# Layers of the second and third chunk as one stream over two chunks of attention, in a transformer and state-space block

## The chip, the core and the metric

The kernel runs on one core of a Trainium2 chip. The core has five engines, each with its own instruction queue: TensorE (PE, matrix products, with weight loads shown apart as PEld), VectorE (DVE), ScalarE (ACT), GpSimd (POOL) and SyncE (SP, which issues most DMAs here). The metric is the device time in microseconds of one execution. The time before is the median of three runs, 1835.65 us.

## The reference

The input `x` has 2 batches of 1024 tokens and 256 features. Four layers follow one another, each on a layer norm of the running sum and added to it:

```python
x = x + attn(layernorm(x), Wq, Wk, Wv, Wo)        # 16 heads of 128, causal, ALiBi, scores clipped
x = x + ternary_ffn(layernorm(x), w_gu, w_pr)     # weights quantised to -1, 0, 1 times a group scale
x = x + mamba(layernorm(x), in_proj, conv, ...)   # 512 channels, 16 states each
x = x + kept_two_ffn(layernorm(x), wg, wu, wd)    # of every 4 hidden values the 2 largest are kept
```

The state-space layer (mamba) projects to 512 channels and a gate, convolves over four tokens, and then computes for every channel and each of 16 states the recurrence `h = exp(delta * A) * h + delta * B * x` along the tokens, and from it `y = sum over states of h * C`. The recurrence runs through all 1024 tokens of a batch.

## The kernel before

**Chunks.** The 2048 tokens are four chunks of 512 (`CH`): the first and second chunk are the two halves of the first batch, the third and fourth those of the second. A chunk has four tiles of 128 queries. Since attention is causal, the first and third chunk have short attention (at most 512 keys) and the second and fourth have long attention (640 to 1024 keys).

**Attention.** `attention()` (L382) is a generator that yields after every score tile: 16 heads by 4 tiles, 64 tiles a chunk. `load_head` (L262) issues a head's loads on SP while the head before it runs; keys and values of a batch's first half are written to DRAM and read back for its second half. `scores` (L355) multiplies queries by keys (L362), clips and masks them (L366, DVE), adds the ALiBi row and finds the minimum (L372, DVE's custom operation), and takes the exponential (L377, ACT). Two tiles later `turn` transposes the result on PE (L293), at a head's end `values` (L304) and `project` (L318, L324) follow. `qkv` (L328) of the next head is traced after the second tile of a head.

**Layers.** `ternary_ffn` (L451), `state_space` (L517) and `kept_two_ffn` (L885) of a chunk are generators too, chained by `rest(k)` (L947). The state space has 4 groups of 128 channels by 16 states, 64 *products* a chunk. Each takes a row of B and a row of C broadcast by DMA on SP, `delta * x * B` on POOL (`enter`, L736), the exponential on ACT (`decay`, L750), the scan along 512 tokens on DVE (`scan`, L757), the multiplication by C on POOL (`weigh`, L771), and an addition into the sum through PE's transposes (`total`, L701). These stages are staggered from one product to the next.

**Order.** A layer generator yields a number, the cost that its author puts on the step, after every step: 3 for a step of the ternary layer, 2.2 for a product, 4 for a step of the last layer, and so on. `cost(k)` (L952) is the sum for a chunk. The driver at the kernel's end (L970) advances attention of chunk `k` by one tile and then traces layers of chunk `k - 1` until their cost has reached the same share of the whole. What is left after the 64th tile is traced before the next chunk begins. So a *stage* is one chunk's attention with the layers of the chunk before it; the first stage has the quantisation of weights instead, and the fourth chunk's layers stand alone in a *tail*. The trace order is a preference: a planner puts each engine's instructions in order by it and by its own estimate of when operands are ready. The scans have one order written out: a scan is put behind the minimum (L372) of the score tile before the last (`pace["front"]`).

The third chunk's last projections (`held`) are not traced in its stage but between matmuls of the tail; the 4 steps of 4 units that `cost` counts for them are never yielded.

Of the kernel before, what the change touches and what calls it, by code (L numbers as in the profile page):

```python
# [17 lines left out]
P = 128  # L18
# [13 lines left out]
NU = S // U  # L32
# [9 lines left out]
def kernel(  # L42
# [28 lines left out]
    def bank(tag, bufs):  # L71
        return lambda name, dt=F32: ps.tile([P, 512], dt, tag=tag, name=name, bufs=bufs)
# [6 lines left out]
    CH = [(b, u) for b in range(B) for u in range(NU)]  # L79
    x = []  # L80
    for k in range(len(CH)):
        x.append(const.tile([P, UT, D], F32, name=f"x{k}"))

    def load_x(k):
        b, u = CH[k]
        src = x_in[b, u * U : (u + 1) * U, :].rearrange("(t p) d -> p t d", p=P)
        if k:
            nc.sync.dma_start(out=x[k], in_=src)
        else:

            for t in range(0, UT, 2):
                (nc.scalar if t else nc.sync).dma_start(out=x[k][:, t : t + 2, :], in_=src[:, t : t + 2, :])
# [19 lines left out]
    def layernorm_T(k, key, put, bank):  # L112
# [4 lines left out]
        step = 2 if k == len(CH) - 1 and key[0] != "a" else UT  # L117

        def turn_two(i):
            if i and step == 2:  # L120
                fill_in()
            tp = bank(f"lnp_{key}_{i}").rearrange("p (c t) -> p c t", c=KC)
            for j in range(2):
# [9 lines left out]
            put(slice(i * P, (i + 2) * P), tp)  # L133

        for i in range(UT):
# [3 lines left out]
            if (i + 1) % step == 0:  # L139
# [3 lines left out]
                for j in range(done.start, done.stop, 2):  # L143
                    turn_two(j)

    def plain(pool, key):
        xT = pool.tile([P, KC, U], F32, tag="xT", name=f"xT_{key}")
# [79 lines left out]
    def normed(k):  # L227
        xns[k], put = plain(a2, f"a{k}")
# [33 lines left out]
    def load_head(k, h):  # L262
        b, u = CH[k]
# [8 lines left out]
        n = (u + 1) * U  # L272
# [7 lines left out]
        if u:  # L280
            kd, vd = kept.pop((b, h))
            nc.sync.dma_start(out=w["kT"][:, :U], in_=kd)
            nc.sync.dma_start(out=w["v_all"][:, :UT, :], in_=vd)
        return w

    def turn(k, h, j, s, st):

        qi = CH[k][1] * UT + j
# [9 lines left out]
    def values(k, h, st):  # L298
        u = CH[k][1]
        zp = ps_z(f"z_{k}_{h}")  # L300
        last = (u + 1) * UT - 1
        for kb in range(last + 1):
            q0 = max(0, kb - u * UT) * P
# [4 lines left out]
        st["z"] = a2.tile([P, U], F32, tag="z", name=f"zs_{k}_{h}")  # L308
        nc.any.tensor_copy(st["z"], zp)  # L309

    def project(k, h, st):

        rr = a3.tile([P, UT], F32, tag="rr", name=f"rr_{k}_{h}")
        nc.vector.reciprocal(rr, st["rs"])
        for t in range(0, UT, 2):
# [12 lines left out]
    def qkv(k, h, st, xT):  # L328
        u = CH[k][1]
        st["qT"] = a2.tile([P, U], F32, tag="qT", name=f"qT_{k}_{h}")  # L330
        kT = st["kT"][:, u * U : (u + 1) * U]
        for n, dst, scale in (("q", st["qT"], -1.0 / math.sqrt(DH)), ("k", kT, 1.0)):
            pp = ps_mm(f"p{n}_{k}_{h}")
# [714 lines left out]
```

## Time and profile before

| what | value |
|---|---|
| median of three runs | 1835.65 us (1833.6 to 1840.51) |
| profiled execution, first to last instruction | 1836.9 us (its own time; the page lists nothing outside this span) |
| PE, DVE, ACT, POOL busy | 1718.3, 1218.3, 963.7, 832.2 us |
| first chunk's attention with quantisation | 0 to 225 us |
| second chunk's attention, first chunk's layers | 225 to 727 us, PE busy 480.3 |
| third chunk's attention, second chunk's layers | 727 to 1119 us, PE busy 354.2 |
| fourth chunk's attention, third chunk's layers | 1119 to 1604 us, PE busy 461.4 |
| tail, fourth chunk's layers | 1604 to 1837 us, PE busy 212.4 |
| POOL's two multiplications of a product (L736, L771) | 1356 and 1428 ns in the mean |
| DVE's scan (L757) | 1210 and 1269 ns |

Busy time is the time in which an engine executes something. Matrix products are pipelined, so PE's busy time counts the time with at least one in flight. The granted clock is a share of PE's full speed, and a window's figure is the mean over it. The stage ends were read off the score tiles and the layers' first and last instructions; a stage's work overlaps its neighbours' by a few microseconds.

### The profile page before, as it was taken

How to read it: one execution, taken by the hardware profiler on the slowest of the kernel's cores; microseconds unless marked ns; L12 is line 12 of the kernel's file. 1: busy time of each engine (PE TensorE's matmuls, PEld its weight loads, DVE VectorE, ACT ScalarE, POOL GpSimd, SP SyncE). 2: the span in 40 equal slices, each digit the busy share in tenths (PEclk: the TensorE clock that was granted, in tenths of full speed). 3: DMA queues.
4: the chain of work that ended last, by engine and by line, in shares of the span. 5: the costliest groups of instructions: out<-in, count | busy, mean ns of one | idle time of the engine just before them, and what ended most of it. 6: DMA issues, size and time to landing. Idle time of an engine off the chain costs nothing. (4 is left out here: it accounts for less than half of the span.)

```text
span 1836.9 us, 24217 instructions
## 1 busy us (share of the span) xinstructions
PE 1718.3 (94%) x7956; PEld 1144.2 (62%) x7956; DVE 1218.3 (66%) x2349; ACT 963.7 (52%) x1789; POOL 832.2 (45%) x674
## 2 busy tenths in 40 slices
PE   7999999998999999998888999999999999998899
PEld 4666666555656557755555667756656565566895
DVE  5666555777785473458886565557788655667975
ACT  3444474656563553555554545566555446446742
POOL 3324032588892000419998000418898500035870
PEclk9999999999999999999999999999999999999999
DMA  6443512466662311337787324227665430212541
GB/s 201 128 142 128 193 46 88 149 203 204 216 202 91 103 52 48 125 109 232 245 247 224 116 71 141 82 67 228 226 214 184 142 115 26 75 53 86 178 136 57
DMA packets 178301, 255.99 MB, mean 139 GB/s; under 512 B 16240, under 2 KB 90992, under 8 KB 177152
## 3 DMA queue, kind: packets, MB, share of 16 engines
q1 hardware_dynamic: 176752, 241.61, 41.4%
q0 software_dynamic: 1152, 12.58, 1.9%
q8 instruction: 63, 1.03, 0.2%
q14 instruction: 62, 0.51, 0.1%
q10 hardware_dynamic: 272, 0.26, 0.0%
HBM read 232.04 MB, written 22.35 MB: 138 GB/s over the span
## 5 line engine op out<-in xcount | busy, mean ns | idle before, releaser
L771 POOL TENSOR_TENSOR hc<-hs,cs 128x512 f32<-128x512 f32 x256 | 362.1, 1428 | 10.8 <-DVE ss L366 3.1
L362 PE MATMUL s<-kT,qT 128*128 128x512 f32 (+3 forms) x768 | 302.7, 495 | 19.9 <-DVE ss L366 18.0
L377 ACT ACTIVATE ss<-ss,nm 128x128 f32<-128x128 f32 (+7 forms) x256 | 198.8, 776 | 183.5 <-DVE nm L372 174.1
L366 DVE SCALAR_TENSOR_TENSOR ss<-s,lower 128x512 f32<-128x512 f32 (+3 forms) x384 | 204.6, 549 | 121.0 <-PE s L362 119.4
L736 POOL TENSOR_TENSOR db<-du,bs 128x512 f32<-128x512 f32 x192 | 259.2, 1356 | 44.4 <-DVE hs L757 30.6
L304 PE MATMUL z<-pT,v 128*128 128x512 f32 (+3 forms) x768 | 264.5, 492 | 10.9 <-ACT pT L296 10.2
L372 DVE CUSTOM_DVE_ANT_0 ss<-ss,alibi 128x128 f32<-128x128 f32 (+7 forms) x256 | 241.3, 945 | 3.5
L750 ACT ACTIVATE da<-dl,a_neg 128x512 f32<-128x512 f32 x256 | 177.9, 698 | 115.6 <-DVE hs L757 90.6
L304 PEld LDWEIGHTS z<-pT,v 128*128 128x128 f32 x768 | 142.8, 190 | 145.1 <-issue 92.7
L296 ACT COPY pT<-pt 128x512 f32<-128x512 f32 (+3 forms) x321 | 145.4, 474 | 162.0 <-PE pt L293 160.4
L293 PE MATMUL pt<-ident,ss 128*128 128x128 f32 x1152 | 180.3, 279 | 32.1 <-DVE x L324 18.5
L293 PEld LDWEIGHTS pt<-ident,ss 128*128 128x128 f32 x1152 | 140.0, 142 | 94.7 <-DVE x L324 33.0
L362 PEld LDWEIGHTS s<-kT,qT 128*128 128x128 f32 x768 | 127.9, 193 | 84.1 <-issue 43.4
L757 DVE TENSOR_TENSOR_SCAN hs<-da,db 128x512 f32<-128x512 f32 x128 | 153.8, 1210 | 38.6 <-ACT da L750 20.8
L757 DVE TENSOR_TENSOR_SCAN hs<-da,carry,db 128x512 f32<-128x512 f32 x128 | 159.1, 1269 | 24.4 <-POOL hc L771 14.7
L324 DVE SCALAR_TENSOR_TENSOR x<-o,rr,x 128x256 f32<-128x256 f32 x256 | 108.9, 476 | 76.7 <-PE o L318 76.5
L701 PE MATMUL y<-ident,hc 128*128 128x128 f32 x1024 | 144.8, 279 | 8.4 <-POOL hc L771 8.4
L342 PEld LDWEIGHTS pv<-wv,xT_a 128*128 128x128 f32 x1024 | 124.4, 192 | 37.1 <-issue 25.3
L342 PE MATMUL pv<-wv,xT_a 128*128 128x128 f32 x1024 | 125.8, 275 | 5.5 <-ACT zs L309 3.4
L701 PEld LDWEIGHTS y<-ident,hc 128*128 128x128 f32 x1024 | 121.0, 145 | 14.3 <-POOL hc L771 11.9
L318 PE MATMUL o<-wo,zs 128*128 128x256 f32 x512 | 125.4, 386 | 4.1 <-ACT kT L338 3.0
L335 PE MATMUL pq<-xT_a,wq 128*128 128x512 f32 x256 | 122.7, 601 | 0.7 <-ACT xT_a L148 0.7
(204 smaller groups left out, 2468.7 us busy)
## 6 DMA issues: line engine op xcount, KB each, us to landing
cs<-bcd SPq DMA_DIRECT2D x256, 256.0 KB, 3.8
bs<-bcd SPq DMA_DIRECT2D x192, 256.0 KB, 4.3
alibi<-alibi_d SPq DMA_DIRECT2D x32, 512.0 KB, 4.2
wq<-in_wqT_dram SPq DMA_DIRECT2D x64, 128.0 KB, 3.5
wk<-in_wkT_dram SPq DMA_DIRECT2D x64, 128.0 KB, 3.1
wv<-in_wvT_dram SPq DMA_DIRECT2D x64, 128.0 KB, 2.8
wo<-in_woT_dram SPq DMA_DIRECT2D x64, 128.0 KB, 2.8
alibi<-alibi_d SPq DMA_DIRECT2D x32, 256.0 KB, 3.6
```

The costliest lines, as they stand in the source:

```text
L293: nc.tensor.transpose(tp[:, i, :], s[:, (kb0 + i) * P : (kb0 + i + 1) * P], ident)
L304: nc.tensor.matmul(zp[:, q0:], lhsT=st["v_all"][:, kb, :], rhs=st["pts"][kb // 4][:, kb % 4, q0:], start=(kb == 0), stop=(kb == last),)
L342: nc.tensor.matmul(vp[:, t, :], lhsT=xT[:, c, t * P : (t + 1) * P], rhs=st["v"][:, c, :], start=(c == 0), stop=(c == KC - 1),)
L362: nc.tensor.matmul(sp[:, :n], lhsT=st["qT"][:, j * P : (j + 1) * P], rhs=st["kT"][:, k0 : k0 + n], start=True, stop=True,)
L366: nc.vector.scalar_tensor_tensor(s[:, k0 : k0 + n], sp[:, :n], CLIP, lower[:, S - W + k0 : S - W + k0 + n], op0=ALU.min, op1=ALU.max,)
L372: pace["tile"] = nc.vector.tensor_tensor_reduce(out=s[:, :W], in0=s[:, :W], in1=st["alibi"][:, :W], scale=1.0, scalar=3.0e38, op0=ALU.add, ...
L377: nc.scalar.activation(s[:, :W], s[:, :W], AF.Exp, bias=nm, scale=-1.0, accum_out=st["rs"][:, j : j + 1])
L701: nc.tensor.matmul(yTs[c][:, t * P : (t + 1) * P], lhsT=h[:, t * P : (t + 1) * P], rhs=ident, is_transpose=True, start=start and t == 0, s ...
L736: nc.gpsimd.tensor_tensor(db[i], du, brow.pop(i), ALU.mult)
L750: nc.scalar.activation(da[i], parts[c][0], AF.Exp, scale=a_neg[:, c, n : n + 1])
L757: nc.vector.tensor_tensor_scan(out=hs[i], data0=da.pop(i), data1=db.pop(i), initial=0.0 if first else carry[:, n, c : c + 1], op0=ALU.mult ...
L771: nc.gpsimd.tensor_tensor(hc[i], hs.pop(i), crow.pop(i), ALU.mult)
```

## The change

A product of the second, third and fourth chunk yields 3.5 in place of 2.2 (the first chunk's still 2.2), and `cost` counts it so. The layers of the first chunk are traced as before. The layers of the second and third chunk form one list, `units`, that is worked off across the third and the fourth chunk's attention without a break between them. Each of these two attention chunks takes a share of the summed cost in proportion to `work(k)`, a weight of its attention that grows with the number of keys: 16 x 228 for the third and 16 x 388 for the fourth. What is not traced when the third chunk's attention ends stays in the list. After the fourth chunk the list is emptied.

The rest of the diff writes chunks as (batch, first tile, number of tiles), so that widths follow the chunk; all four chunks keep four tiles. Keys and values of a batch's first half go to rows of one DRAM tensor as wide as the batch, in place of one that is as wide as the chunk. `normed` of the next chunk and `qkv` of the next head change places in the text; they are traced after different tiles.

```diff
-    CH = [(b, u) for b in range(B) for u in range(NU)]
+CH = [(b, t, UT) for b in range(B) for t in range(0, NT, UT)]
...
-        if u < NU - 1:
-            kd = dr.tile([P, U], F32, tag="kd", name=f"kd_{k}_{h}", bufs=H)
-            nc.sync.dma_start(out=kd, in_=kT)
...
+        if t0 + ut < NT:
+            if t0 == 0:
+                kept[b, h] = (
+                    dr.tile([P, S], F32, tag="kd", name=f"kd_{b}_{h}", bufs=H),
+                    dr.tile([P, NT, DH], F32, tag="vd", name=f"vd_{b}_{h}", bufs=H),
+                )
+            kd, vd = kept[b, h]
+            nc.sync.dma_start(out=kd[:, t0 * P : t0 * P + w], in_=kT)
+            nc.sync.dma_start(out=vd[:, t0 : t0 + ut, :], in_=v)
...
                 if i >= 0:
-                    yield 2.2
+                    yield PRODUCT(k)
...
+    PRODUCT = lambda k: 2.2 if k == 0 else 3.5
+
     def rest(k):
-        yield from ternary_ffn(k)
-        yield from state_space(k)
-        yield from kept_two_ffn(k)
+        part = CH[k][2] / UT
+        for layer in (ternary_ffn, state_space, kept_two_ffn):
+            for step in layer(k):
+                yield step * part
...
+    work = lambda k: H * sum(32 + 10 * (CH[k][1] + j + 1) for j in range(CH[k][2]))
+    units, done, later = [], 0.0, range(2, len(CH))
+
+    def layers(until):
+        nonlocal done
+        while units and done < until:
+            step = next(units[0], None)
+            if step is None:
+                units.pop(0)
+            else:
+                done += step
+
     for k in range(1, len(CH)):
-        r, done = rest(k - 1), 0.0
-        for i in range(H * UT):
+        units.append(rest(k - 1))
+        if k == 1:
+            share = cost(0)
+        else:
+            share = sum(cost(i - 1) for i in later) * work(k) / sum(work(i) for i in later)
+        begun, steps = done, H * CH[k][2]
+        for i in range(steps):
             next(heads)
-            whole = cost(k - 1)
-            while done < whole * (i + 1) / (H * UT):
-                done += next(r, whole)
-        for _ in r:
-            pass
+            layers(begun + share * (i + 1) / steps)
+        if k in (1, LAST):
+            layers(math.inf)
```

## The prediction

> **What bounds the kernel now.** I read the page's head first, then the busy times in windows cut at the stage ends (an attention chunk is a stage), then the windows inside the third and fourth chunk's attention, then how many score tiles lie in each, and last the groups and waits of the worst window.
>
> ```profile
> span 1836.9 us, 24217 instructions
> PE 1718.3 (94%) x7956; PEld 1144.2 (62%) x7956; DVE 1218.3 (66%) x2349; ACT 963.7 (52%) x1789; POOL 832.2 (45%) x674
> PE   7999999998999999998888999999999999998899
> POOL 3324032588892000419998000418898500035870
> ...
> 727.00:1119.00 392.00, 354.16 (x1617) 240.18 (x1616) 257.39 (x486) 199.76 (x399) 203.70 (x162) 0.97 0.52 165
> 1119.00:1604.00 485.00, 461.37 (x2017) 292.16 (x2015) 320.41 (x603) 267.36 (x459) 224.99 (x171) 0.99 0.43 139
> ...
> 727.00:830.00 103.00, 99.98 (x432) 64.57 (x430) 54.87 (x136) 55.40 (x109) 32.20 (x31) 1.00 0.34 113
> 830.00:1005.00 175.00, 141.91 (x709) 101.13 (x710) 143.53 (x209) 93.09 (x194) 169.24 (x130) 0.93 0.78 240
> 1005.00:1119.00 114.00, 112.27 (x477) 74.47 (x476) 58.99 (x142) 51.27 (x98) 2.26 (x2) 1.00 0.29 96
> 1119.00:1239.00 120.00, 118.35 (x481) 74.06 (x479) 66.94 (x144) 70.40 (x114) 31.68 (x33) 0.97 0.29 95
> 1239.00:1455.00 216.00, 198.45 (x965) 130.93 (x964) 174.70 (x308) 125.58 (x227) 190.28 (x136) 1.00 0.65 209
> 1455.00:1604.00 149.00, 144.57 (x575) 87.17 (x573) 78.77 (x154) 71.38 (x118) 3.03 (x3) 1.00 0.21 71
> ```
>
> In the window rows the columns are length, then busy us (and instructions) of PE, PEld, DVE, ACT and POOL, then clock, DMA share and GB/s. PE is busy for 94% of the span, and four of the six small windows have it at 97 to 99%. The hole is 830 to 1005, where the second chunk's state space runs beside the third chunk's short attention: PE idles 33.1 us of 175, its clock is granted at 0.93, and POOL is at 97%. The stretch 1239 to 1455 does the same products beside the long attention and loses 17.6 us; there no engine is full (PE 92%, POOL 88%, DVE 81%).
>
> ```profile
> L771 POOL TENSOR_TENSOR hc<-hs,cs 128x512 f32<-128x512 f32 x64 | 85.4, 1339 | 2.7 <-DMA cs<-bcd 2.7
> L736 POOL TENSOR_TENSOR db<-du,bs 128x512 f32<-128x512 f32 x60 | 81.2, 1356 | 2.3 <-DMA bs<-bcd 2.3
> L757 DVE TENSOR_TENSOR_SCAN hs<-da,carry,db 128x512 f32<-128x512 f32 x61 | 76.7, 1271 | 15.3 <-POOL hc L771 13.9 <-ACT da L750 1.4
> PE y L701 <- POOL hc L771: 7.9, 7, 3.0
> PE pt L293 <- DVE x L324: 8.0, 6, 2.4
> ```
>
> So in 830 to 1005 POOL's two multiplications per product set the pace, and PE waits for them (7.9 us) or for DVE, which does the scans ahead of the residual updates (8.0 us).
>
> **The change part by part.**
>
> *Trace order.* The layers of a chunk are units of cost given out per attention tile (64 tiles a stage). Before, the second chunk's layers cost 2.2 x 69 + 150.8 = 302.6 units, 4.73 per tile, which is 2.15 products per tile. The 150.8 are 35 (ternary layer), 30 (state space up to its products), 9 and 8 (inside and after them), 68.8 (last layer). With 3.5 per product the two chunks cost 392.3 and 395.8. The attention's weights are 16 x 228 and 16 x 388, so the third chunk's attention takes 37% of 788.1, or 291.7 units (4.56 per tile), and the fourth's 496.4 (7.76 per tile). The products thus go at 4.56 / 3.5 = 1.30 per tile beside the third chunk and 2.22 beside the fourth (before 2.16). The 65 units ahead of them take 14.3 tiles beside the third chunk (before 13.7; the trace has 16 score tiles up to 830, 30 in the hole, 18 after). At the end of that stage 217.7 units, 62 products, are issued, 57 of them added up. The rest of the second chunk's layers, about 100 units, moves into the first 13 tiles of the fourth chunk's attention.
>
> *Third chunk's attention.* The front stays 103 us with 16 tiles. The product stretch has 48 tiles in place of 30. A tile of short attention costs PE at most 150.6 / 46 = 3.27 us (60 to 215 us of the first chunk, with some weight transposes in it); I take 3.2. A product costs (141.9 x 0.93 - 30 x 3.2) / 64 = 0.56 us of PE. So PE: 48 x 3.2 + 57 x 0.56 = 186 us. POOL: 62 x (1.339 + 1.356) + 8 = 175. DVE: the attention rows of the window give 2.14 us a tile (custom operation 0.97, mask 0.47, update 0.45, small ones 0.25), 48 x 2.14 + 62 x 1.271 + 15 for step sizes = 197. Three engines come close together. PE at the 92% of 1239 to 1455 gives 202; DVE at the 97% that POOL reached gives 203. I take 203. Ends: 190 (PE at the 98% of 1005 to 1119) and 224 (DVE at the 88% that POOL had in the balanced stretch). Stage: 103 + 203 = 306 in place of 392, **-86 us**.
>
> A row speaks against the spreading. The score tile's custom operation (two SBUF inputs) took 1049 ns at 128x512 in the hole and 692 ns in 1005 to 1119, where POOL was idle; over the four widths the excess is 0.48 us, and 48 tiles now meet it in place of 30. It is inside the 2.14. The Trainium skill, "SBUF — State Buffer", section "Who interferes with whom", says that a VectorE instruction with two SBUF inputs and a GpSimd one that reads SBUF exclude each other for a whole instruction. As an estimate from that page, were every tile to wait out one whole POOL operation of 1.34 us, DVE would need 0.86 x 48 = 41 us more, the stretch 238 and the kernel 1847; the row has a third of that wait.
>
> *Fourth chunk's attention.* Moved in: window 1005 to 1119 less its attention, 112.3 - 18 x 3.2 = 54.7 us of PE, and seven products' additions, 4: **+58.5 us**, at the 98% that this work had. Its DVE (comparisons, masks) and one POOL power lie beside attention. Then the third chunk's layers start at tile 13 and run denser. Products are as dense as before (2.22 against 2.16), so that stretch keeps its loss. Their front, 65 units, has 8.4 tiles where it had 13.7: PE work 8.4 x 5.3 (a long tile: (198.5 - 34) / 31) + 48.8 (103 window less 16 tiles) = 93 us, and the same chain was done in 103 us from 727 to 830, so the products may lag some 10 us, two tiles. The third chunk's last projections are held for the tail, which leaves 16 units, two tiles, unused at the end. I take **+3 us**; ends 0 and +30 (a lag of six tiles more).
>
> *What else is issued.* The last layer's three weight loads (1 MB each, 4.9 to 9.9 us) and the ternary layer's two (8.7 and 11.7 us, POOL's queue) move behind the fourth chunk's head loads, and the row requests of the last products lie on SP between them. A head is loaded one head ahead, 24 to 30 us (four tiles of 392 / 64 or 485 / 64), which hides landings of 3 to 5 us; uncovered, a head's start would slip by that once or twice. The ternary loads still wait for the last layer's buffers, now beside attention. The third chunk's normalisation for the fourth (one 1.0 us POOL power) now queues behind products: 0 to 3 us, taken in the 203. Keys and values go to rows of one larger tensor, 2.3 and 2.5 us a write and 3.0 and 3.6 a read in as many requests: 0, hidden by the same lead. The widths by chunk, slices and the order of two calls on different tiles issue nothing new: 0. First two stages and tail: 0.
>
> **Sum.** 1836.9 (the profiled execution; the page shows nothing around the span, and it is 1.25 above the median) - 86 + 58.5 + 3 = 1812.4, so **1812**; the difference to the median is a tenth of a per cent and I leave it.
>
> **Rivals.**
> *Nothing but PE left (faster).* The long product stretch reaches 190 and the dense layers cost nothing: 1812 - 13 - 3 = 1796. For: windows at 98 to 99% wherever POOL is free. Against: three engines within 11 us of each other.
> *DVE takes POOL's place (no change).* The stretch takes 224: 1812 + 21 = 1833. For: the waits "PE pt <- DVE x" and the 81% balanced stretch that loses 17.6 us. Against: fewer scans per tile than in either stretch of before.
> *The dense fourth stage (slower).* The third chunk's layers, squeezed into 51 tiles, fall behind: with the lag beyond the two spare tiles, each further tile leaves work to be done after attention, where nothing covers it, at a long tile's 5.3 us. Six such tiles, +32, and 1844; from five tiles on the kernel is level with before. For: the chain's 103 us against 93. Against: attention tiles can be issued ahead in between.
>
> **How the numbers follow.** My forecast 0.50, the faster rival 0.20, level 0.16, slower 0.14. A change of 0.5% (9.2 us) is about what a measurement of this kernel tells from none. Faster: 0.70; same: 0.16; slower: 0.14. The likeliest case alone spans 1800 to 1824. For 8 in 10 the range takes in the faster rival and its unknowns down to 1788 and the level one up to 1840.
>
> **What the new profile would show.** The third chunk's attention ends near 1034, with about 48 tiles beside products, POOL at 85 to 90%, PE near 92% and fewer half-clock stretches. The fourth takes about 546 us, its first 13 tiles beside the second chunk's last layer, and products again at seven us a tile with PE near 92%. The prediction is wrong if DVE passes 95% in the long stretch, if PE idles ahead of the third chunk's products, or if layer work stands after the last attention tile.

## The result, and the profile after

The changed kernel takes 1849.88 us in the median (1847.15 to 1854.09, four runs), beside 1836.68 us of the kernel before (1833.6 to 1840.51) measured with it: a ratio of 1.0072, 95% interval 1.0053 to 1.0091. It is slower by 0.7%; 1812 us and a gain of 1.3% were forecast. The profiled execution took 1847.15 us, its span is 1845.4 us, so 33.0 us of the span are to be explained against the sum of 1812.4.

The head of the changed kernel's page, and its windows cut as those of before were (length, then busy us and instructions of PE, PEld, DVE, ACT and POOL, then clock, DMA share, GB/s):

```profile
span 1845.4 us, 24241 instructions
PE 1713.0 (93%) x7956; PEld 1140.7 (62%) x7956; DVE 1232.5 (67%) x2359; ACT 954.8 (52%) x1778; POOL 827.4 (45%) x674
PE   7999999998999999997988899999888999898899
POOL 3333031588891000408778500135987740035970
...
725.00:1057.00 332.00, 293.14 (x1410) 200.37 (x1409) 237.60 (x441) 177.62 (x372) 199.39 (x159) 0.98 0.58 182
1057.00:1614.00 557.00, 519.52 (x2224) 329.66 (x2222) 356.24 (x658) 280.82 (x475) 224.83 (x175) 0.99 0.39 128
...
830.00:1057.00 227.00, 190.74 (x961) 132.93 (x960) 180.76 (x289) 121.03 (x262) 171.79 (x132) 0.97 0.70 218
...
1272.00:1490.00 218.00, 190.25 (x896) 124.80 (x895) 168.34 (x290) 117.72 (x214) 183.31 (x133) 0.98 0.63 201
```

The work has moved as the change meant it to. The third chunk's attention takes 332 us in place of 392, the fourth's 557 in place of 485; together they are 12 us longer, and the first two stages and the tail are 4 us shorter. The other parts of the diff are at work in the second chunk's stage too, and that takes 495 us, 496 before: they are not what costs. POOL's row shows the saturated "9998" of the third chunk spread out to "8778". But nothing was won: in the long product stretch beside the third chunk, 830 to 1057, no engine is near full (PE 84%, DVE 80%, POOL 76%), and in the stretch beside the fourth chunk PE has fallen from 92% to 87%.

To compare stretches whose work differs I use one number of my own, the *loss*: the length of a stretch less the usual time of its matmuls. A product stretch runs from the first scan of a chunk to its last multiplication by C; what lies ahead of it in the stage is the front, what lies behind it the rear. The usual time of a matmul is the distance from its start to the next one's, read off the trace of before where the next follows at once (429 ns for 128x512, 216 ns for 128x256, 109 to 112 ns for 128x128; 230 and 120 ns for the faster number format). The stage borders are the last attention instructions here, a few us later than in the windows. The losses are good to some tenths of a us, the counts of score tiles to one.

| us | kernel before | kernel after |
|---|---|---|
| third chunk's stage: matmuls | 329.7 | 278.9 |
| its loss: front, products, rear | 4.2 + 51.3 + 3.1 = 58.6 | 5.9 + 47.4 + 0.5 = 53.8 |
| fourth chunk's stage: matmuls | 445.9 | 496.7 |
| its loss: front, products, rear | 7.0 + 24.1 + 7.7 = 38.8 | 5.1 + 38.3 + 12.2 = 55.6 |
| length of the two product stretches (score tiles) | 179.2 (30), 215.3 (31) | 228.3 (48), 224.7 (29) |

So 50.8 us of PE's work moved from the third stage to the fourth, and the loss went down by 4.8 us in the one and up by 16.8 us in the other. The 51 us of loss that the change was to win back stayed almost whole, though POOL was relieved. The loss contains time that PE worked at half clock: in the third chunk's product stretch 23.9 us stand at half clock before and 13.7 after, in the fourth's none and 6.8. If half of that time is lost, which is an estimate, the losses without it are 39 and 41 us in the third stage and 24 and 35 in the fourth; the little that the third stretch won would be clock. Whom PE waited for in the long stretch (waits of PE alone, us in total, times, longest):

```profile
PE z L312 <- ACT pT L304: 11.0, 5, 6.7
...
PE pt L301 <- ACT pT L304: 4.6, 1, 4.6
PE pt L301 <- DVE x L333: 4.6, 3, 2.1
PE pt L301 <- ACT ss L390: 3.9, 4, 1.3
```

The wait for POOL, "PE y <- POOL hc", was 7.9 us before and is gone; only a weight load still waits 0.4 us for that tile. In its place PE waits for the attention's own chain: transposed probabilities, exponentials and the residual. The same list for the stretch beside the fourth chunk, 1272 to 1490, and below it the two rows of 1239 to 1455 of the kernel before:

```profile
DVE ss L379 <- PE s L375: 40.6, 8, 10.9
...
POOL db L754 <- DVE hs L775: 19.9, 3, 6.9
```

```profile
DVE ss L366 <- PE s L362: 9.0, 11, 3.3
...
PE s L362 <- DVE ss L366: 7.8, 8, 1.3
```

There DVE now stands still for up to 10.9 us at a time until PE makes the next scores, 40.6 us in all against 9.0, with as many products and as dense as before. POOL's wait for the scans hardly changed (19.9 us, 17.1 before). Two questions follow: what holds PE in the long stretch if not POOL, and why equally dense products cost 14 us more beside the same long attention.

### The profile page after: what moved, and what is told of

It is laid out like the page before. It is cut to its first block, busy times and chain, and to the rows that moved or that the text cites. A ratio compares the mean times of both kernels' runs of the same rounds, so it can differ in the third digit from the quotient of the medians.

```text
span 1845.4 us, 24241 instructions
## 1 busy us (share of the span) xinstructions
PE 1713.0 (93%) x7956; PEld 1140.7 (62%) x7956; DVE 1232.5 (67%) x2359; ACT 954.8 (52%) x1778; POOL 827.4 (45%) x674
## 4 chain that ended last, share of the span: by engine, by line
PE 61%; DVE 16%; issue 8%; POOL 7%; ACT 4%; DMA 3%; SPq 0%; POOLq 0%; DVEq 0%; ACTq 0%
PE z L312 10%; PE s L375 7%; PE pv L352 5%; DVE hs L775 5%; PE pq L345 4%; PE pk L345 4%; PE o L327 4%; PE pt L301 3%; DVE ss L385 3%; PE in L626 3%; PE g_g L456 3%; PE u_g L456 3%; POOL hc L789 3%; DVE ss L379 3%; POOL db L754 2%
## 5 line engine op out<-in xcount | busy, mean ns | idle before, releaser
L789 POOL TENSOR_TENSOR hc<-hs,cs 128x512 f32<-128x512 f32 x256 | 356.1, 1408 | 41.2 <-PE y L719 30.9
L385 DVE CUSTOM_DVE_ANT_0 ss<-ss,alibi 128x128 f32<-128x128 f32 (+7 forms) x256 | 251.0, 983 | 3.8 <-DMA alibi<-alibi_d 0.3
```

Source lines behind the costliest of these rows:

```text
L385: pace["tile"] = nc.vector.tensor_tensor_reduce(out=s[:, :W], in0=s[:, :W], in1=st["alibi"][:, :W], scale=1.0, scalar=3.0e38, op0=ALU.add, ...
L789: nc.gpsimd.tensor_tensor(hc[i], hs.pop(i), crow.pop(i), ALU.mult)
```

## The experiments

"After" and "before" in the edits say which kernel was edited. Ratios are to the kernel before, measured beside it, with the 95% interval.

### The two halves of the change, and how the work is shared out

**The stream alone (after, edited).** Products weigh 2.2 everywhere again.

```diff
-    PRODUCT = lambda k: 2.2 if k == 0 else 3.5
+    PRODUCT = lambda k: 2.2
```

> The changed kernel with 2.2 per product everywhere: one stream over the third and fourth chunk's attention, products as cheap as before. Units: 302.6 + 304.8 = 607.4, of which the third chunk's attention takes 37%, 224.8 (3.51 per tile, 1.60 products per tile; 65 units of front take 18.5 tiles, so 45 tiles with products) and the fourth 382.6 (5.98 per tile, 2.72 products per tile). Theory 'spreading does not pay' (PE loses about as much per product stretch however long it is, and a denser fourth stage loses more): third stage near 335 us, the fourth's product stretch POOL-bound and losing more than 38 us, total 1845 to 1865. Rival 'the weight did the harm' (products held back into more tiles while other layers are squeezed): total 1825 to 1838.

Measured: 1877.03 us, 1.0199 (1.0172 to 1.0226). The third chunk's products lie beside 40 tiles (loss 47.1), the fourth's beside only 22, three to a tile, and there the loss is 62.6 us (37.5 us of the stretch stand at half clock). The total lies 12 us above the expected range; the third stage took 337 us, as expected. The row of that stretch, and its main wait:

```profile
1296.00:1512.00 216.00, 168.87 (x793) 111.98 (x793) 170.21 (x263) 104.04 (x186) 179.87 (x137) 0.91 0.61 193
```

```profile
PE pt L301 <- DVE x L333: 27.7, 4, 12.9
```

**The weight alone (after, edited).** Each chunk's layers are finished in their own stage again; products weigh 3.5.

```diff
-            share = sum(cost(i - 1) for i in later) * work(k) / sum(work(i) for i in later)
+            share = cost(k - 1)
...
-        if k in (1, LAST):
+        if True:
             layers(math.inf)
```

> The changed kernel with each chunk's layers kept to its own stage and emptied at its end, as before, but with 3.5 per product: 392.3 units over 64 tiles, 6.13 per tile, 1.75 products per tile in place of 2.15, the other layers 1.3 times as dense. Theory 'spreading does not pay': the third stage's product stretch takes more tiles (37) and more time, but its loss of some 50 us stays, so 1834 to 1842, level with before. Rival 'POOL's saturation is what cost PE': the stretch at 1.75 products per tile frees POOL and PE regains 15 to 25 us there, 1812 to 1825.

Measured: 1855.96 us, 1.009 (1.0072 to 1.0108), above both expected ranges. The second chunk's products are spread over 35 tiles beside the third chunk and lose 60.6 us, more than the 51.3 of 30 tiles; the fourth's over 36 tiles lose 25.9. Stream alone +2.0%, weight alone +0.9%, both +0.7%: the halves do not add up. The weight repairs part of what the stream does, by giving the fourth chunk's products 29 tiles in place of 22.

**Another share (after, edited).** The third chunk's attention takes 43% of the stream in place of 37%.

```diff
+            share = sum(cost(i - 1) for i in later) * {2: 0.43, 3: 0.57}[k]
```

> The changed kernel with one size altered: the third chunk's attention takes 43% of the two chunks' cost in place of 37% (338.9 units, 5.30 per tile, 1.51 products per tile; the fourth 449.2, 7.02 per tile, 2.01 products per tile). Theory 'the fourth stage is too dense': the product stretch beside the fourth chunk's attention covers 34 tiles in place of 29 and its loss of PE falls from 38 to about 25 us, the third's stays at 45 to 52: 1830 to 1840. Rival 'the split does not matter': within 5 us of the changed kernel, 1843 to 1853.

Measured: 1851.6 us, 1.0081 (1.0065 to 1.0097), in the range of "the split does not matter". The third chunk's products lose 46.8 us beside 41 tiles, the fourth's 34.6 beside 31. Between 30 and 48 tiles the third chunk's loss is 47 to 61 us in all of these kernels: how thinly the products are spread there hardly matters. (Two kernels further down, with 44 tiles and an even rhythm, lose 37 and 39 us.)

**Thinner products beside the fourth chunk (after, edited).** Only the third chunk's products weigh more, and the third stage keeps its share.

```diff
+    PRODUCT = lambda k: (2.2, 3.5, 4.5, 3.5)[k]
...
+            share = 291.7 if k == 2 else cost(1) + cost(2) - 291.7
```

> The changed kernel with 4.5 per product for the third chunk's layers alone, and the third chunk's attention keeping its 291.7 units: beside the fourth chunk's attention 566.4 units, 8.85 per tile, so 1.97 products per tile in place of 2.22, while the other layers there are 14% denser. Up to the fourth chunk's attention it is the changed kernel. Theory 'density of products in the fourth stage': its stretch loses 25 in place of 38 us, in all 1833 to 1842. Rival 'density of the other layers': the stretch gains what the front and the last layer lose, 1846 to 1858.

Measured: 1865.31 us, 1.0157 (1.0136 to 1.0179), above both expected ranges. With 31 tiles in place of 29 the fourth chunk's products lose 43.7 us, more than the 38.3 of the denser order, and 16.5 us are lost ahead of them. 20.5 us of that stretch stand at half clock (6.8 in the changed kernel); by the estimate above, 33 and 35 us are left without it. So thinner products alone do not bring the loss back to 24 us. (The second stage of this run was 7 us longer than that of the changed kernel with the same instruction order, which I cannot explain; the losses beside the fourth chunk don't contain it.)

### What holds PE in the long stretch

**DVE's second SBUF input (one edit, in both kernels).** The score tile's custom operation adds the ALiBi row and finds the minimum, from two SBUF inputs. Here a plain reduction with one input takes its place; the ALiBi row is left out of the computation.

```diff
-        pace["tile"] = nc.vector.tensor_tensor_reduce(
-            out=s[:, :W], in0=s[:, :W], in1=st["alibi"][:, :W], scale=1.0,
-            scalar=3.0e38, op0=ALU.add, op1=ALU.min, accum_out=nm,
-        )
+        pace["tile"] = nc.vector.tensor_reduce(nm, s[:, :W], AX.X, ALU.min)
```

In the kernel before:

> The kernel before, with the ALiBi row left out: the minimum of a score tile is taken by a reduction with one SBUF input in place of the custom operation with two. It serves as the base of the next run. Stretch of the second chunk's products: DVE's durations there should lose their excess of some 26 us. Theory 'exclusion of DVE and POOL': 1790 to 1815. Rival 'order of the queues': 1815 to 1835.

In the changed kernel:

> The changed kernel with the same ALiBi row left out. Theory 'exclusion of DVE and POOL costs the long stretch' (48 tiles meet POOL in place of 30, DVE's excess there 35 us against 26): without it the change gains, 15 to 30 us less than the kernel before without the row, and the third chunk's product stretch falls from 227 to about 200 us. Rival 'the queues' bursts' (score tiles of a head and scans take turns on DVE, POOL and PE wait in turns): the difference to the kernel before without the row stays between -5 and +20 us and the stretch at 215 us or more.

Measured: 1812.56 us, 0.9857 (0.9835 to 0.9878), with the kernel before edited, and 1818.07 us, 0.9887 (0.9864 to 0.991), with the changed one edited. The first lies in the range of the exclusion; the second lies 5.5 us behind it and its stretch at 213 us, between what the two theories said. Groups of the changed kernel in its long stretch, the custom operation with its 512 and 128 columns (count, busy us, mean ns), below them the same tiles with the reduction, and last the custom operation in 1005 to 1119 of the kernel before, where POOL is idle:

```profile
L385 DVE CUSTOM_DVE_ANT_0 ss<-ss,alibi 128x512 f32<-128x512 f32 x12 | 14.5, 1204 | 0.2
...
L385 DVE CUSTOM_DVE_ANT_0 ss<-ss,alibi 128x128 f32<-128x128 f32 x11 | 10.0, 905 | 0.3
```

```profile
L385 DVE TENSOR_REDUCE nm<-ss 128x1 f32<-128x512 f32 x12 | 8.1, 674 | 0.2
...
L385 DVE TENSOR_REDUCE nm<-ss 128x1 f32<-128x128 f32 x11 | 3.1, 281 | 0.2
```

```profile
L372 DVE CUSTOM_DVE_ANT_0 ss<-ss,alibi 128x512 f32<-128x512 f32 x5 | 3.5, 692 | 0.3
...
L372 DVE CUSTOM_DVE_ANT_0 ss<-ss,alibi 128x128 f32<-128x128 f32 x4 | 1.2, 293 | 0.1
```

With POOL idle the custom operation itself took 692 and 293 ns, so the reduction is only 2 to 4% cheaper, and nearly all of the difference (0.53 and 0.62 us here, 0.48 and 0.53 at the two widths between) is what the second input costs DVE beside POOL's work. I call it the exclusion of DVE and POOL. It makes 14 us for 30 tiles at 0.48 us and 25 for 47 at 0.53, not the 26 and 35 of the expectations. POOL's own multiplications change little: 1328 and 1360 ns beside the custom operation, 1296 and 1284 beside the reduction. The long stretch shrinks from 228 to 213 us (loss 47.4 to 32.3):

```profile
823.00:1036.00 213.00, 194.58 (x970) 137.46 (x971) 155.33 (x245) 121.18 (x263) 166.45 (x134) 0.95 0.68 213
1251.00:1467.00 216.00, 196.33 (x936) 130.65 (x935) 162.03 (x270) 120.64 (x220) 167.46 (x136) 0.98 0.60 187
```

In the kernel before, the short stretch only goes from 179 to 175 us (49.3 of loss left). So this exclusion costs 15 us in the long stretch of the changed kernel and 4 us in the full one of before (11 us in the kernel before beside the fourth chunk). It doesn't explain the fourth stage: there the stretches lose 13.4 us in the edited kernel before and 30.4 in the edited changed one, a difference of 17 against the 14 of the originals.

**Half of one POOL multiplication taken out (one edit, in both kernels).** `weigh` multiplies half of the tokens, and PE adds that half twice; the other half of the sum over states is left out.

```diff
-                nc.gpsimd.tensor_tensor(hc[i], hs.pop(i), crow.pop(i), ALU.mult)
+                    nc.gpsimd.tensor_tensor(hc[i][:, : w // 2], h[:, : w // 2], cr[:, : w // 2], ALU.mult)
...
-                        lhsT=h[:, t * P : (t + 1) * P], rhs=ident,
+                        lhsT=h[:, (t % 2 if half else t) * P : ((t % 2 if half else t) + 1) * P], rhs=ident,
```

In the kernel before:

> The kernel before with the multiplication by C over half of the tokens, as in the run with the changed kernel. POOL in the third chunk's stretch falls from 169 to about 130 us of 175. Theory 'POOL's saturation is only a small part of what PE loses there' (the waits that name POOL were 7.7 of 33 us): the stretch shrinks from 179 by 8 to 20 us, the other two by 4 to 8 us each, in all 1805 to 1822. Rival 'POOL's saturation was the whole loss': the stretch shrinks by 25 us or more, below 154, in all below 1805.

In the changed kernel:

> The changed kernel with the multiplication by C over half of the tokens (PE adds the half twice), which takes some 0.64 us of POOL per product away and leaves the scans whole. Theory 'chain on DVE': POOL's time is worth little, only the part in which it excludes DVE: third chunk's stretch 215 to 225 us, in all 1825 to 1842. Rival 'POOL still sets the pace of the products, through its buffers': third chunk's stretch below 212, fourth's below 212 us, in all below 1820.

Measured: 1813.14 us, 0.986 (0.984 to 0.9879), with the kernel before edited; 1824.27 us, 0.9917 (0.9893 to 0.994), with the changed one edited; the first as the theory had it, the second, with 213 us for its stretch, between theory and rival. The third chunk's product stretch of before, then the third's and the fourth's of after, with the lighter `weigh`:

```profile
822.00:988.00 166.00, 143.38 (x733) 104.01 (x733) 139.99 (x212) 95.49 (x196) 136.63 (x133) 0.93 0.84 260
```

```profile
831.00:1044.00 213.00, 189.41 (x970) 131.13 (x971) 171.29 (x292) 122.60 (x264) 139.34 (x134) 0.98 0.76 233
1258.00:1473.00 215.00, 193.40 (x937) 127.42 (x936) 167.73 (x299) 120.44 (x220) 149.52 (x137) 1.00 0.63 206
```

In the kernel before POOL loses a fifth of its time in the hole (169 to 137 us) and is no longer full (82%), yet the stretch only gets 13 us shorter and keeps 38.3 of its 51.3 us of loss. More than that POOL's saturation was not worth. In the changed kernel, where POOL stood idle for a quarter of the stretch, the same edit gives 15 us (47.4 to 32.4). A POOL that is far from full costs as much here as a full one. That DVE and PE wait their turn behind single POOL instructions would explain it, but was not tested by itself. Beside the fourth chunk the difference between the kernels falls from 14 to 9 us.

**Half of the scans taken out (one edit, in both kernels).** The scan runs over half of the tokens; `weigh` reads that half twice.

```diff
-                        out=hs[i], data0=da.pop(i), data1=db.pop(i),
+                        out=hs[i][:, : w // 2], data0=da.pop(i)[:, : w // 2], data1=db.pop(i)[:, : w // 2],
```

In the kernel before:

> The kernel before with the same half scans. Theory 'chain on DVE': its second and fourth chunk's stretches gain as in the changed kernel (12 and 10 us), the third chunk's little, since POOL's 169 us stay as the floor of its 175: 1805 to 1822, that is 5 to 20 us more than the changed kernel with half scans, so that the change would pay. Rival: it gains as much as the changed kernel or more and stays faster.

In the changed kernel:

> The changed kernel with the scans of the first three chunks over the first half of the tokens alone (the multiplication by C reads that half twice, so POOL, PE and ACT keep their work): DVE gets some 0.6 us per product less. Theory 'PE waits for the score tiles' chain on DVE, behind the scans': the product stretches (losses 24, 47 and 38 us) lose 12, 20 and 15 us less, in all 1790 to 1812, and the third chunk's falls from 228 to 205 us or less. Rival 'no single engine, any order does': less than 15 us in all, 1832 or more.

Measured: 1833.13 us, 0.9967 (0.9946 to 0.9989), with the kernel before edited, and 1836.0 us, 0.9985 (0.9972 to 0.9997), with the changed one edited: the chain on DVE was expected to give far more in both, and in the kernel before the third chunk's stretch even grew, from 179 to 184 us. DVE falls to 65% in the long stretch, which still loses 40.2 us:

```profile
825.00:1046.00 221.00, 195.45 (x972) 137.26 (x973) 143.11 (x297) 120.49 (x260) 173.96 (x133) 0.95 0.70 223
```

DVE's load is thus no bound there either: 38 us less work on it give 7. (23.9 us of that stretch stand at half clock in place of 13.7, so some 5 us of the gain went into clock.) Beside the fourth chunk the kernels lose 21.5 and 37.3 us, 16 apart.

**The transposes one tile later (after, edited).** `turn` follows its scores by three tiles in place of two, so that PE asks later for what ACT and DVE make.

```diff
-LAG = 2
+LAG = 3
```

> The changed kernel with a score tile's transposes three tiles after its scores in place of two (value products and projection one tile later as well): the chain of mask, minimum, exponential and copy gets one tile more, 4.4 us beside short attention. Theory 'latency of the chain': the waits of value products and transposes for it (some 20 us in the third chunk's stretch) shrink by half or more, 1822 to 1840. Rival 'buffers': score tiles, transposed tiles and the v buffer are held longer, and it is level or slower, 1845 to 1880.

Measured: 1893.69 us, 1.0293 (1.0274 to 1.0313), above both expected ranges. The first chunk's stage, where no products run, grew by 42 us; the long stretch lost 10 us less. The windows of the two:

```profile
0.00:279.00 279.00, 239.38 (x1028) 151.15 (x1029) 145.80 (x423) 106.38 (x265) 63.20 (x78) 0.96 0.42 132
892.00:1110.00 218.00, 194.15 (x975) 137.01 (x974) 180.78 (x299) 120.79 (x264) 173.46 (x133) 0.96 0.73 228
```

So the waits for the attention's chain are worth about 10 us in the long stretch and the edit is no cure. Whether the gains of exclusion, POOL's instructions and the chain add up was not tested. No single edit brought the loss of this stretch below 32 us, and what makes up the rest was not isolated.

### Why the fourth chunk's stretch got worse

**The next head's projections one tile later (one edit, in both kernels).** If the extra loss came from `qkv` and the products falling on the same tiles, moving the one should move the loss.

```diff
-            if j == ut // 2 - 1 and
+            if j == ut // 2 and
```

In the changed kernel:

> The changed kernel with the next head's query, key and value projections traced one tile later (after the third tile of a head), so that they no longer follow the head's value products in one block of PE work, 8 to 12 us without a score tile. Theory 'bursts': DVE no longer runs dry behind that block (pauses of 9 to 11 us before a mask, once in two heads), the product stretches lose 10 to 25 us less in all, 1822 to 1838. Rival 'the block is not the cause': 1843 to 1860, the projections come later and the next head's first scores wait for them.

In the kernel before (there the tile's number is 1, and becomes 2):

> The kernel before with the same move of the projections by one tile. Theory 'bursts': it gains too in its product stretches (losses 25, 51 and 24 us), 1815 to 1832; if it gains as much as the changed kernel, the block is a cost of both and not what the change lost. Rival: 1833 to 1850.

Measured: 1878.07 us, 1.0225 (1.0207 to 1.0244), and 1871.6 us, 1.0199 (1.0175 to 1.0224), both above all that was expected. All product stretches lose 1 to 9 us more in both kernels, and the difference beside the fourth chunk stays at 14 us (46.1 against 32.2). It tells nothing of the difference; the theory of one collision with the projections fell.

**The phase.** What was left was the order itself. A head has four tiles, and products come in groups of 16, one for each block of 128 channels, with one step of 3 units between. In the kernel before, a group costs 16 x 2.2 + 3 = 38.2 units; at 4.76 a tile (304.8 units of the third chunk's layers on 64 tiles) that is 8.0 tiles, two heads, and each group begins at the same place, 1.65 tiles after a head does (65 units ahead of the first make 13.65 tiles). In the changed kernel it costs 59 units; at 7.76 a tile that is 7.6 tiles, and its place drifts, from 1.35 to 0.2. Time, tiles and loss of each eight products (half a group) beside the fourth chunk, read off the two traces:

| kernel | us / tiles / loss of each eight products |
|---|---|
| before | 20/4/2.4, 32/4/3.9, 25/4/1.8, 32/4/4.6, 25/4/1.7, 32/4/4.6, 25/4/2.1, 22/2/2.6 |
| after | 20/3/3.9, 28/3/6.2, 34/5/5.0, 23/2/4.3, 36/5/5.2, 26/3/7.0, 36/5/3.8, 15/2/3.1 |

Four kernels tell density, drift and place apart. First, before with products at 2.4 in place of 2.2, so that the groups drift a little (8.3 tiles each, beginning at 1.05, 1.4, 1.7 and 2.0):

```diff
-                    yield 2.2
+                    yield 2.4
```

> The kernel before with 2.4 per product in place of 2.2 (in its costs too): 318.8 units a stage, 4.98 per tile, products 2.08 per tile in place of 2.16, and a group of 16 products with its step sizes takes 41.4 / 4.98 = 8.3 tiles in place of 8.0, so that it no longer falls on two heads. Theory 'rhythm' (the kernel before gains from a channel group every two heads, 8 products a head; any other pace makes the queues' order irregular): the second and fourth chunk's stretches lose 30 to 38 us each in place of 24, in all 1843 to 1862. Rival 'density': thinner products cost less, the stretches lose 20 to 24 us, 1830 to 1838.

Measured: 1855.78 us, 1.009 (1.0066 to 1.0113). The loss beside the fourth chunk is 28.5 us (before 24.1), beside the second 28.5 (24.9), beside the third 60.2 (51.3). The total is in the range of "rhythm", the losses beside the second and fourth chunk lie just below its 30 to 38.

Then the changed kernel with weights and share that make a group last 8.0 tiles again, so that it doesn't drift, but begin 3.2 tiles after a head does:

```diff
+    PRODUCT = lambda k: (2.2, 3.5, 3.524, 3.5)[k]
...
+            share = 314.7 if k == 2 else cost(1) + cost(2) - 314.7
```

> The changed kernel with its pace set to whole heads: the third chunk's attention takes 314.7 units (4.92 per tile; a group of 16 products takes 59 / 4.92 = 12.0 tiles, three heads), the fourth the rest, with 3.524 per product of the third chunk (7.42 per tile; a group takes 59.4 / 7.42 = 8.0 tiles, two heads). Theory 'rhythm': the fourth chunk's stretch loses about 24 in place of 38 us, the third's 35 to 47 in place of 47: 1818 to 1837. Rival 'the dense fourth stage, whatever its pace': losses stay at 34 us or more there, 1843 to 1855.

Measured: 1850.75 us, 1.0066 (1.0049 to 1.0083). The stretch loses 41.7 us: an even rhythm is not enough.

```profile
1266.00:1492.00 226.00, 197.11 (x910) 127.87 (x909) 172.60 (x295) 121.02 (x218) 190.22 (x136) 0.98 0.62 196
```

Next, the kernel before with the same density and rhythm, but its products two tiles later in the head (at 3.6):

```diff
-                    yield 2.2
+                    yield 2.53
...
-                yield 4
+                yield 24
```

(The 24 stand on the last step ahead of the products. `cost` counts both, which keeps 2.15 products to a tile and a group at 8.0 tiles beside the fourth chunk.)

> The kernel before with 20 units added ahead of the first product and 2.53 per product in place of 2.2 (costs too): 347.9 units a stage, 5.44 per tile, a group of 16 products in (16 x 2.53 + 3) / 5.44 = 8.0 tiles as before and 2.15 products per tile as before, but beginning at tile 15.6 in place of 13.7, so two tiles later within a head. Theory 'phase' (the rhythm of two heads helps only where the groups' ends fall at the right tile of a head): the second and fourth chunk's stretches lose 35 us or more each in place of 24, in all 1855 to 1875. Rival 'any rhythm of whole heads will do': 22 to 27 us each, 1833 to 1846.

Measured: 1896.9 us, 1.0302 (1.0273 to 1.0331). Beside the second chunk the loss goes from 24.9 to 44.2 us, beside the fourth from 24.1 to 40.4, beside the third from 51.3 to 66.5; the third's stretch and the fourth's have 33 and 32 tiles in place of 30 and 31. The losses are as "phase" had them; the total lies 22 us above its range. The fourth's stretch, and whom the engines wait for there:

```profile
1289.00:1527.00 238.00, 210.91 (x983) 138.58 (x982) 173.07 (x317) 126.87 (x227) 187.14 (x133) 0.97 0.57 180
```

```profile
DVE ss L366 <- PE s L362: 50.4, 13, 11.3
POOL db L736 <- DVE hs L757: 28.6, 8, 12.3
```

Nothing of the change is in this kernel, and yet it shows the changed kernel's picture: DVE stops for up to 11.3 us for the next scores (9.0 us in all in the kernel before, 40.6 in the changed one). Last, the changed kernel with even groups that begin 1.6 tiles into a head, as in before:

```diff
+    PRODUCT = lambda k: (2.2, 3.5, 3.007, 3.5)[k]
...
+            share = 314.7 if k == 2 else 408.9
...
-                done += step
+                done += step * (0.79 if third[0] and not third[1] else 1.0)
```

(`third` holds the third chunk's layers and whether their first product has been traced; what lies ahead of it counts at 0.79.)

> The kernel paced to whole heads (three heads a group beside the third chunk's attention, two beside the fourth's) with the phase of the kernel before: all that comes ahead of the third chunk's products beside the fourth chunk's attention is counted at 0.79 of its cost, and its products at 3.007 (408.9 units, 6.39 per tile), so that products begin at tile 17.6 in place of 19.2, at the same tile of a head as before (13.7). Theory 'phase': that stretch loses 22 to 28 us in place of 42, in all 1828 to 1840, level with the kernel before or just faster. Rival 'the dense stage': 35 us or more, 1845 to 1858.

Measured: 1832.15 us, 0.9965 (0.9948 to 0.9981): faster than the kernel before by a third of a per cent, and than the changed one by 1%. The two stages, the fourth chunk's product stretch, and a wait of it:

```profile
734.00:1061.00 327.00, 298.97 (x1448) 206.44 (x1447) 238.14 (x457) 176.14 (x369) 204.00 (x161) 0.98 0.58 188
1061.00:1601.00 540.00, 508.51 (x2172) 321.42 (x2171) 350.80 (x647) 280.92 (x471) 221.96 (x172) 0.99 0.40 131
...
1258.00:1466.00 208.00, 187.03 (x893) 123.71 (x894) 170.79 (x297) 118.36 (x214) 187.72 (x136) 0.98 0.67 213
```

```profile
DVE ss L379 <- PE s L375: 8.7, 13, 3.3
```

The fourth chunk's stretch loses 30.1 us (38.3 in the changed kernel, 41.7 with the other place; 22 to 28 were expected), and DVE's wait for scores is back at 8.7 us. After the first eight products, which lose 8.7 us, the others lose 1.0 to 5.5 us, where those of before lose 1.7 to 4.6. The third chunk's stretch, 44 tiles, loses 39.0 us in place of 47.4; since the kernel with groups at 3.2 has 36.8 there too, that part comes with the share of 314.7 units, which the two have in common, not from the place beside the fourth chunk. Beside the fourth chunk this kernel loses some 20 us less than the one with groups at 3.2, 12 of them in the product stretch; the other 8 lie in the front and the rear, whose layers are spread differently too.

So the place of the product groups within a head decides: with 2.11 to 2.16 products to a tile in the trace order and groups of two heads, a start at 1.6 tiles lost 24 and 30 us, a start at 3.2 or 3.6 tiles 42 and 40 (without half of the half-clock time 24 and 25 against 37 and 34). That is shown from both sides, in the kernel before and in the changed one. The executed order agrees: from the second eight on, the first scan of each eight products starts 0.95 to 1.15 tiles after a head's first exponential in the kernel before and in this one (in tiles of that chunk's exponentials), 1.4 to 2.6 in the even kernel that begins at 3.2, and 2.2 to 3.3 in the shifted one; in the changed kernel it falls anywhere from 0.15 to 4.0.

Three things stay open. The changed kernel's own places, 1.35 to 0.2, were not held one by one, so that its 14 us come from them is a conclusion from the others. The place matters less where products are thin: the run with the weight alone has 1.77 products to a tile beside the fourth chunk and groups of 9.5 tiles that begin all over a head, and loses 25.9 us. And what in the queues makes one place good was not isolated. DVE's long stops for scores are no measure of it, since that run has more of them than the changed kernel (40.6 us):

```profile
DVE ss L379 <- PE s L375: 52.5, 11, 10.9
```

## Why the prediction was wrong

- **"POOL's two multiplications per product set the pace": wrong in size.** The step took a full engine for the one that held PE. The waits that it quoted already said otherwise: "PE y <- POOL hc" was 7.9 us of 33.1 idle. Taking a fifth of POOL's time away brings 13 us of the 51 (179 to 166). What was read right is that this wait goes: none of the 7.9 us is left.
- **The third chunk's product stretch, "I take 203": measured 227, the largest miss, 24 us.** The step set the stretch at the time of the busiest engine (DVE at 97%). Its terms were close: PE busy 191 (186 predicted), POOL 172 (175), DVE 181 (197), 47 to 48 tiles (48). But no engine reached 85%. Of these three engines, which hand short instructions to one another, none filled up; PE stood idle for 36 us of the window (227 less 191) where the sum left 17. What makes up most of that stayed open: no single edit brought the loss below 32 us. ("Three engines within 11 us of each other" was a slip: 175 to 197 is 22.) The rival "DVE takes POOL's place" named the size (224), but not the cause: DVE stands at 80%, and not at the 88% from which 224 was made.
- **The row that spoke against the spreading was underweighted.** Its excess, 0.48 us a tile, came out at 0.51, 0.47, 0.52 and 0.61 us for the four widths, 0.53 in the mean. The prediction put that time on DVE alone, inside the 2.14 us a tile. The run without the second input shows that it reaches PE: 15 us of the 228. The Trainium skill, "SBUF — State Buffer", section "Who interferes with whom", has the exclusion, and the estimate of 238 us from it was above the 228 measured. The section also says that PE never waits on anyone for a port. For ports no run here contradicts it; PE pays all the same, most likely through what DVE hands it late.
- **The front, 103 us: right** (105).
- **"Products are as dense as before, so that stretch keeps its loss": wrong, and this turned level into slower.** The density is indeed the same, but the loss went from 24.1 to 38.3 us. The run with thinner products (43.7) and the shifted kernel before (40.4) show that the loss can rise with the density the same or lower; another place of the groups in a head moved it by 12 to 16 us. The prediction had the dense front in mind (+3, ends 0 and +30), and the front lost less than before (5.1 against 7.0). The rear lost 4.5 more.
- **Moved work, +58.5 us: 50.8** by the matmuls' usual time. (The step's own terms, 54.7 and 4, make 58.7, and 60 at the 98% that it names.)
- **The slower rival, "the dense fourth stage" with 1844 us, was near in time and wrong in mechanism.** The third chunk's products begin at the fourth chunk's tile 22, as computed, and no layer work stands behind the last tile.
- **First two stages and tail, 0:** -3.5 us together in the profiled execution.

The misses add up: 26 us in the third stage, 10.5 in the fourth (the loss too low by 14, the moved work and window edges the other way), less 3.5 elsewhere, together the 33.0.

## What to carry to other kernels

An engine that is full in a window is not yet the engine that the bound one waits for: add up the waits that name it before its relief is credited with the whole loss, and expect the next chain in their place. Such a sum is a guide and no bound: POOL was named for 7.9 us and its relief won 13, and in the changed kernel, where PE no longer named it, 15. Where three engines at 75 to 85% exchange short instructions, do not set a stretch at the busiest one's time; take the loss of a stretch already measured in that state. And where two streams are traced into one static order, the place and rhythm of the one within the period of the other is a parameter of its own: a changed share or weight shifts it unasked, so work it out from the costs beforehand (here 8.0 against 7.6 tiles to a group) and tune it in whole periods.

## What the runs showed of the hardware

Taking away a fifth of POOL's time shortened the product stretch as much where POOL was busy 76% (15 us) as where it was busy 97% (13 us).

PE's clock was granted at half speed without a long pause of PE. In the kernel before, PE is busy for 20.0 of these 22 us (the windows overlap by two), and the clock still falls to 0.72 in the second:

```profile
1160.00:1170.00 10.00, 8.84 (x56) 7.30 (x54) 2.63 (x4) 5.75 (x10) 7.84 (x7) 0.98 0.09 26
1168.00:1180.00 12.00, 11.16 (x60) 10.21 (x60) 5.56 (x16) 1.89 (x4) 2.70 (x2) 0.72 0.04 12
```

The half-speed stretch begins at 1169.5 us, and the longest pause of PE in the 6.8 us ahead of it is 0.8 us. The Trainium skill, "TensorE: Matmul & The Clock Gate", section "What's actually happening", names an idle window of some 3.4 us as the condition; here two pauses of 0.3 and 0.8 us and the first of eight matmuls with a single column stand in the 3.4 us ahead of it, and which of them brought the clock down no run shows. Over the span the half-speed time is 41 us before, 34 after, and 100 in the kernel before with its products two tiles later.
